# Layers 1 and 2 of a four-layer graph network: another way to the layer norm's scale, a shorter lag, x1 read in pieces; in layer 0, the guess and the diffusion at another place

## The chip, the core and the metric

The kernel runs on one core of one Trainium2 chip. A core has five engines that work side by side, each with its own queue of instructions: TensorE (PE, matrix products; its weight loads have their own queue, PEld), VectorE (DVE), ScalarE (ACT), GpSimd (POOL) and SyncE (SP). SP and POOL issue the DMAs here: SP plain loads and stores, POOL gathers of rows by an index. The metric is the time of one launch on the device in microseconds (us). All times below are in us, counted in a trace from the start of the span, unless marked ns.

## The reference

4096 nodes with 256 features each, and a sparse matrix `adj` (4096 x 4096, a few non-zero entries in a row, the diagonal among them). Four layers, each of the form x = x + layer(relu(layer_norm(x))). Cut to what matters:

```python
# layer 0: two steps of attention (top-p over 4096 logits a row) and of diffusion
for n in range(2):
    A = top_p_attention(Xa, W1, W2, W3)
    Xf = R @ Xf                       # R: adj + I, rows normalised
    Xa = A @ Xa
    Z = Z + Xf @ U1[n].T + Xa @ U2[n].T
out0 = layer_norm(X + Z)
# layer 1: graph convolution
adj_norm = (adj + I) / rowsum
out1 = tanh(adj_norm @ (h @ W) + b)
# layer 2: graph attention with four heads over the non-zero entries
Wh = (h @ W.T).reshape(n, 4, 64)
e = leaky_relu(score_l[:, :, None] + score_r.T[None], 0.2)
alpha = softmax(where(mask, e, -inf), axis=2)
out2 = elu(alpha @ Wh)
# layer 3
out3 = relu(adj @ (h @ weights))
```

The layer norm of a row is (x - mean) / sqrt(var + 1e-5). The kernel applies it as relu(scale * x + shift), with scale = (var + 1e-5) ** -0.5 and shift = -mean * scale.

## The kernel before

The nodes lie in `NB` = 32 blocks of `P` = 128. A block sits with its nodes on the 128 partitions. In the sparse products of layers 1 to 3 a block of targets reads its neighbours in `CHUNKS` = 5 gathers of 128 rows each (`gather`, L835), and PE multiplies them by a compact piece of the matrix, `ac` (`sparse_product`, L850 and L854).

**Order.** On DVE, ACT and PE the program order is the order of execution in the parts considered here (`manual_schedule`). On POOL and SP a scheduler orders the instructions.

**Layer 0** (L793 to L1875). `front` (L1028) computes the normalised input, keys and the moments of the keys. `guess` (L972) is a generator that turns these moments into a first guess of the threshold of every row (`minus_guess`), in pieces that are asked for one at a time: some pieces are a PE product with a DVE operation (list: `near` times `mk`), others four small products, and the last ones short DVE operations (L993 ff). Then `layer0_step(n, ...)` (L1116) gives a `period(b)` for one block of targets. Its text is the table `ORDERS[n]` (L1094): each word is a call, `word@k` a call for block b + k. In a period the logits of block b + 3 (`logits0`, `exps0`: ACT exponentials L1162 with `minus_guess` as their offset), the search for the threshold of block b + 2 (signs, `s1` to `s3`: ACT L1178; updates `r0` to `r3` and `first`: DVE L1190, L1208, L1229), the cut of block b (`below` L1331, `cut` L1393, `drop` L1400, all DVE over 128x4096) and the attention of block b (`flip` PE L1440, `take` ACT L1446, `attend` PE L1455) stand side by side. The word `fill` takes as many pieces of a generator as the tuple `pieces` says for this period (L1853, L1867); periods -3 to -1 are the prologue, in which only b + 2 and b + 3 exist. In step 1 the generator also holds the lists of columns (`listed_columns`, from L794).

In step 1 the diffusion runs as well. `pair(b)` (L1671) names the two blocks which period b mixes: k = 0, the first diffusion, for b = 0 to 15, and k = 1, the second, for b = 17 to 32. `opened` (L1700) starts the gathers of each (`reach`), `mix0` and `mix1` are the sparse products (PE L850, `pr<-vg,ac`), `mixed0` stores a pair (`mixed_d`, L1567) from which the second diffusion gathers. `stood` to `tabled` form layer 1's table `v_d` from the finished blocks; `x1` is stored to `x1_d`.

**Layer 1** (L1877 to L2048). `xr` holds x1 for all 32 blocks and is kept to the end. It is read in eight pieces ahead of everything else of the layer; then the bias and the weights, among them `w_gat`, whose last eight columns DVE computes from tiles of a pool `heads` that closes before the layer's own pools open. In the loop (L2011) a block b is loaded and gathered, and PE forms its sparse product; `y` (DVE L2034), tanh (ACT L2037) and the addition into `xr` follow. Behind it come the class `Projection`'s steps for block o = b - `LAG`, with `LAG` 5: `stats` (mean and variance, and every four blocks the power on POOL, L1934), `shifts` (L1939), `normalise` (ACT relu L1945, PE transposes L1950), `turned` (L1955), `product` (L1961), `store` (`put`, L1986, which writes a block of the table that layer 2 gathers from, through SP).

**Layer 2** (L2050 to L2172). One period per block: `load` gathers five chunks of table rows, `entries(b, k)` forms the factors of a chunk (three heads by ACT, L2079, the fourth by DVE, L2081, then one DVE operation over all four, L2082), `attend` is the product (PE L2097), `attended` copies its sums (ACT L2107), `turned` transposes them, `divided` normalises (DVE L2117, L2119) and takes the exponential for the elu (ACT L2123), `elu` adds to `xr` and takes the stats, and the steps of `Projection` run 8 blocks behind, writing the last layer's table. In a period the exponential stands behind the factors of chunks 0 to 2 and ahead of those of chunks 3 to 5.

**The last layer** (L2186) is a sparse product per block with a relu.

Of the kernel before, what the change touches and what calls it, by code (L numbers as in the profile page):

```python
# [63 lines left out]
F32 = mybir.dt.float32  # L64
# [12 lines left out]
P = 128  # L77
# [577 lines left out]
def fast_layers(  # L655
# [445 lines left out]
    keys@-1 exps1@3 xa_pe@-1 s0@3 mark r0@3 drop copy_xa@-1 s3@2 store_xa@-1 flip0 mark flip1 mark  # L1101
    take0 h_pe@-1 take1 first r3@2 flip2 attend0 mark mark attend1 store_h@-1 take2 flip3 take3 fill
    """,
# [3 lines left out]
    exps1@3 stood@-3 cut mix0 s0@3 laid@-3 s3@2 projected@-3 finish@-1 level@-2 mixed0 drop mix1 tabled@-3  # L1107
    r0@3 r3@2 attend7@-1 shifted@-2 first flip0 spread0 flip1 take0 heads@-1 other1 s1@3 attend0 take1 r1@3 flip2 flip3
    take2 attend1 take3 flip4 attend2 flip5 fill
# [16 lines left out]
    def layer0_step(n, va, kt, own, extra=None):  # L1126
# [544 lines left out]
        def pair(b):  # L1671

            k, i = (0, b) if b < NB // 2 else (1, b - NB // 2 - 1)
            return [(2 * i + r, k) for r in range(2)] if n == 1 and 0 <= b and 0 <= i < NB // 2 else []
# [25 lines left out]
        def opened(b):  # L1700
            if n == 0 and 0 <= b < NB:
                state[b]["adj"] = load_adj(extra, b)
            if n == 1 and b in (0, NB // 2):
                reach(0, b // (NB // 2))
                reach(1, b // (NB // 2))
            if n == 1:
                other(b, 0)
                if 0 < b <= NB:
                    loaded(b - 1, "base", base_d, 1)
                for d in two_ends(b - 1):  # L1710
                    loaded(d, "xb", x, 2)
# [75 lines left out]

        def period(b, fill=(), pieces=(0, 0, 0)):


            pieces = iter(pieces)
            for name, off in tables[max(b - NB + 1, 0)]:
                if name == "fill":
                    some(fill, next(pieces))
                else:
                    calls[name](b + int(off))
# [42 lines left out]
    with ExitStack() as st:  # L1839
# [13 lines left out]
        with tc.manual_schedule(engines=MANUAL):  # L1853
            period, verify, close = layer0_step(0, h0, kt0, own, adj_pool)
            for b in range(-3, NB):
                period(b, guesses, {-3: (3, 0, 0), -2: (3, 9, 9)}.get(b, (0, 0, 0)))
            lists = listed_columns(marks, e_pool.tile([P, N], F32, name="e"), ps)
            guesses = close(lists)

    with ExitStack() as st:  # L1860
# [3 lines left out]
        with tc.manual_schedule(engines=MANUAL):  # L1864
            period, verify, close = layer0_step(1, va1, kt1, s1, vg_pool)
            fill = by_turns(guesses, lists)
            pieces = {-3: (6, 0, 0), -2: (6, 4, 1), -1: (0, 2, 99)}  # L1867
            for b in range(-3, NB + 2):
                period(b, fill, pieces.get(b, (0, 0, 0)))
                if b == -1:  # L1870
# [10 lines left out]
    MANUAL = {ENGINES.DVE, ENGINES.Activation, ENGINES.PE}  # L1881
    GROUP = 4

# [5 lines left out]

    res = ctx.enter_context(tc.tile_pool(name="res", bufs=1))  # L1890
    xr = res.tile([P, NB, D], F32, name="xr")
    for q in range(8):
        bs = slice(q * NB // 8, (q + 1) * NB // 8)
        nc.sync.dma_start(xr[:, bs, :], blocks(x1_d)[:, bs, :])

# [6 lines left out]

    bias = across(res, gcn_b, "bias")
    w_last = weights(res, last_w, "w_last")

    w_gat = res.tile([P, DC, D + 2 * HEADS], F32, name="w_gat")
    nc.sync.dma_start(w_gat[:, :, :D], gat_wt.rearrange("(c p) m -> p c m", p=P))
    with tc.tile_pool(name="heads", bufs=1) as hp:
        for k, a_d in enumerate((gat_al, gat_ar)):
            a_all = across(hp, a_d, f"a_all{k}")  # L1910
            prod = hp.tile([P, DC, HEADS, DK], F32, name=f"prod{k}")
            for c in range(DC):
                nc.vector.tensor_mul(prod[:, c].rearrange("p h d -> p (h d)"), w_gat[:, c, :D], a_all)
                nc.vector.tensor_reduce(
                    w_gat[:, c, D + k * HEADS : D + (k + 1) * HEADS], prod[:, c], AX.X, ALU.add
                )

    class Projection:


        def __init__(self, sm, wk, ps, w, put, width=D):
            self.sm, self.wk, self.ps, self.w, self.put, self.width = sm, wk, ps, w, put, width
            self.tiles = {}

        def stats(self, b):

            six = self.sm.tile([P, 6], F32, name="six")
            nc.vector.bn_stats(six, xr[:, b, :])
            nc.vector.bn_aggr(spread_[:, b, :], six)
            if b % GROUP == GROUP - 1:  # L1930
                bs = slice(b + 1 - GROUP, b + 1)
                var = self.sm.tile([P, GROUP], F32, name="var")
                nc.vector.tensor_scalar_add(var, spread_[:, bs, 1], LN_EPS)
                nc.gpsimd.tensor_tensor(scale[:, bs], var, minus_half[:, :GROUP], op=ALU.pow)  # L1934

        def shifts(self, b):
            if b % GROUP == 0:
                bs = slice(b, b + GROUP)
                nc.vector.scalar_tensor_tensor(  # L1939
                    shift[:, bs], spread_[:, bs, 0], -1.0, scale[:, bs], op0=ALU.mult, op1=ALU.mult  # L1940
                )
# [37 lines left out]
    with ExitStack() as st:  # L1979
# [28 lines left out]

        second = Projection(sm, wk, ps, w_gat, put, D + 2 * HEADS)
        LAG = 5  # L2010
        with tc.manual_schedule(engines=MANUAL):  # L2011
            for b in range(NB + LAG + 3):
                o = b - LAG
                if b < NB:
                    ac = adj_pool.tile([P, CHUNKS + 1, P], F32, name="ac")
                    nc.sync.dma_start(ac, adjc_d[b])
                    vg = gathered(adj_pool, v_d[0], b)
                if 0 <= o < NB:
                    second.shifts(o)
                    second.normalise(o)  # L2020
# [31 lines left out]
    with ExitStack() as st:  # L2052
# [4 lines left out]
        ps = st.enter_context(tc.tile_pool(name="gatps", bufs=2, space=PSUM))  # L2057
        third = Projection(sm, wk, ps, w_last, to_table(wk, v_d[1]))
        state = [{} for _ in range(NB)]
        LAG = 8  # L2060

# [8 lines left out]
        def entries(b, k):  # L2070
# [5 lines left out]
            for h in range(HEADS):  # L2076
                by = s["tab"][:, k, HW + h : HW + h + 1]
                if h < HEADS - 1:
                    nc.scalar.mul(u[:, k, h, :], t[:, h, :], by)  # L2079
# [34 lines left out]
        def divided(b):  # L2114
# [5 lines left out]
                s["y"], s["po"][:, :, :DK], rden.to_broadcast([P, HEADS, DK]), op=ALU.mult  # L2120
            )
            s["below"] = wk.tile([P, D], F32, name="below")
            nc.scalar.activation(s["below"], s["y"].rearrange("p h d -> p (h d)"), AF.Exp)  # L2123
# [10 lines left out]
        with tc.manual_schedule(engines=MANUAL):  # L2134
            for b in range(NB + LAG + 2):
# [10 lines left out]
                if 0 <= o < NB:  # L2146
                    third.shifts(o)
                    third.normalise(o)
# [14 lines left out]
                if turning:  # L2163
                    divided(b - 2)
                if entered:
                    for k in range(3, CHUNKS + 1):
                        entries(b, k)
                if 0 <= o - 2 < NB:
                    third.store(o - 2)
# [95 lines left out]
```

## Time and profile before

| | us |
|---|---|
| median of 3 runs (3387.29 to 3389.24) | 3388.16 |
| the profiled execution | 3391.82 |
| its span in the trace | 3390.0 |
| step 0, first to last period | about 161 to 1279 |
| step 1 | 1404 to 2562 |
| layer 1 | 2562 to 2851 |
| layer 2 | 2851 to 3180 |
| last layer | 3180 to 3390 |

The stages are cut by the trace: the first DVE operation L1331 of a step, the last store of `v_d`, the first gather of layer 2 (2851.22) and the first of the last layer (3179.60). Over the span PE is busy 77%, DVE 78%, ACT 66%, POOL 38%; the mean granted PE clock is 0.89 of full.

How such a page is read: a line of a group names the code line, the engine, the operation, out<-in with shapes and the count; then its busy time in us and the mean ns of one; then the idle time of the engine just before these instructions, with what ended it. "issue" is idle time for which the profile shows no wait. Busy shares over the whole span are means over stages that have different limits, so the stages are looked at one by one, with windows (busy time of each engine in a stretch).

### The profile page before, as it was taken

Reading aid. Unit: us, or ns where it says so; the run is one execution under the profiler, and the core shown is the slowest. Engines: PE = TensorE matmul, PEld = TensorE weight load, DVE = VectorE, ACT = ScalarE, POOL = GpSimd, SP = SyncE. Lnnn points to the kernel's source line nnn. Section 1 sums busy time; section 2 is a strip of 40 time slices with the busy share of each in tenths; the row PEclk is TensorE's granted clock in tenths of the full one; section 3 lists DMA queues with packets and bytes.
Section 4 is the critical chain, followed back from the end, with each engine's and each line's share of the span. In section 5 each row is a group of like instructions: output and inputs, shape, how many; then the busy total and the mean of one; then the engine's idle time right before and its main releaser. Section 6 shows DMA issues by size and latency. Waiting matters only on the chain. (4 is left out here: it accounts for less than half of the span.)

```text
span 3390.0 us, 43724 instructions
## 1 busy us (share of the span) xinstructions
PE 2616.5 (77%) x12404; PEld 1964.9 (58%) x12404; DVE 2652.4 (78%) x9355; ACT 2233.8 (66%) x3340; POOL 1280.6 (38%) x1350
## 2 busy tenths in 40 slices
PE   6558788787887878379898989898883576888666
PEld 5335565565565656157676666767662455777543
DVE  3489999999999998879999999999852344888300
ACT  3588888888888862878888888898620113677200
POOL 1000000000000000188888745656554773754376
PEclk9779899899898999689999999999996898889888
DMA  3012222222222222234444422433335563543475
GB/s 116 8 60 72 81 77 72 87 76 70 88 72 76 82 72 66 76 113 123 133 122 124 123 84 84 124 98 120 100 89 190 166 192 90 135 126 108 139 212 166
DMA packets 213847, 357.00 MB, mean 105 GB/s; under 512 B 33879, under 2 KB 147036, under 8 KB 213596
## 3 DMA queue, kind: packets, MB, share of 16 engines
q1 hardware_dynamic: 169100, 237.74, 22.4%
q0 software_dynamic: 43520, 116.14, 13.0%
q8 instruction: 101, 1.65, 0.2%
q14 instruction: 150, 1.23, 0.1%
q10 hardware_dynamic: 976, 0.23, 0.0%
HBM read 290.85 MB, written 63.13 MB: 104 GB/s over the span
## 5 line engine op out<-in xcount | busy, mean ns | idle before, releaser
L1178 ACT ACTIVATE unread<-e,next_pair 128x4096 uint8<-128x4096 f32 (+1 forms) x384 | 1097.0, 2857 | 46.5 <-DVE next_pair L1229 42.6
L1455 PE MATMUL pa<-va,at 128*128 128x256 f32 x2048 | 501.5, 393 | 71.9 <-DVE t L1585 59.3
L1446 ACT COPY at<-pat 128x512 f32<-128x512 f32 x512 | 291.3, 581 | 310.4 <-PE pat L1440 305.2
L1455 PEld LDWEIGHTS pa<-va,at 128*128 128x128 f32 x2048 | 386.6, 196 | 154.9 <-ACT at L1446 59.2
L1455 PE MATMUL pa<-h,at 128*128 128x256 f32 x2048 | 471.1, 380 | 1.0 <-ACT at L1446 0.8
L1440 PE MATMUL pat<-ident,e 128*128 128x128 f32 x2048 | 319.5, 298 | 192.0 <-DVE e L1400 191.7
L1341 POOL COPY eighth<-best 128x16 f32<-128x16 f32 x64 | 21.7, 339 | 1149.4 <-DVE best L1339 929.8
L1440 PEld LDWEIGHTS pat<-ident,e 128*128 128x128 f32 x2048 | 275.9, 156 | 276.1 <-DVE e L1400 219.3
L1339 DVE MAX8 best<-near 128x8 f32<-128x256 f32 x1024 | 404.3, 416 | 3.2
L1455 PEld LDWEIGHTS pa<-h,at 128*128 128x128 f32 x2048 | 376.2, 191 | 49.0 <-ACT at L1446 4.9
L835 POOL DMA_INDIRECT vg<-v_d,column x320 | 306.7, 959 | 139.4 <-issue 89.7
L1148 PE MATMUL pl<-kt,qb 64*128 64x512 f32 x1024 | 280.5, 660 | 89.9 <-ACT e L1162 89.6
L1162 ACT ACTIVATE e<-pl,minus_guess 128x1024 f32<-128x1024 f32 x256 | 283.4, 1115 | 58.1 <-PE pl L1148 57.7
L850 PE MATMUL acc<-vg,ac 128*128 128x256 f32 x768 | 233.9, 452 | 109.0 <-DMA vg<-v_d,column 81.8
L1331 DVE SCALAR_TENSOR_TENSOR near<-e,end_hi 128x4096 f32<-128x4096 f32 x64 | 286.6, 4478 | 0.1
L1393 DVE SCALAR_TENSOR_TENSOR e<-e,end_t 128x4096 f32<-128x4096 f32 x64 | 286.6, 4478 | 0.0
L1400 DVE MATCH_REPLACE8 e<-drop,e 128x4096 f32<-128x4096 f32 x64 | 282.1, 4408 | 0.0
L850 PEld LDWEIGHTS acc<-vg,ac 128*128 128x128 f32 x768 | 162.1, 225 | 176.8 <-DMA vg<-v_d,column 112.3
L2097 PE MATMUL acc<-u,tabg 128*65 128x128 f32 x1536 | 210.4, 293 | 62.4 <-DVE u L2082 61.1
L835 POOL DMA_INDIRECT ac<-in_adjt,adj_row x160 | 238.6, 1491 | 46.5 <-issue 35.5
L835 POOL DMA_INDIRECT vg<-mixed_d,column x160 | 220.2, 1376 | 92.5 <-issue 44.3
L850 PE MATMUL pr<-vg,ac 128*128 128x257 f32 (+1 forms) x768 | 195.4, 405 | 58.5 <-issue 28.4
(543 smaller groups left out, 4543.9 us busy)
## 6 DMA issues: line engine op xcount, KB each, us to landing
adj<-in_adjt SPq DMA_DIRECT2D x128, 512.0 KB
ac<-adjc_d SPq DMA_DIRECT2D x96, 384.0 KB
adjc_d<-ac SPq DMA_DIRECT2D x32, 384.0 KB
vg<-v_d SPq DMA_DIRECT2D x64, 128.0 KB
targets<-steep_d SPq DMA_DIRECT2D x32, 256.0 KB
vg<-v_d,column POOLq DMA_INDIRECT x320, 3.6
table_d<-tab SPq DMA_DIRECT2D x32, 132.0 KB
tabg<-table_d SPq DMA_DIRECT2D x32, 132.0 KB
```

The lines of the kernel that those rows point to most:

```text
L835: nc.gpsimd.indirect_dma_start(out, None, rows, bass.IndirectOffsetOnAxis(ap=index, axis=0))
L850: nc.tensor.matmul(acc, ac[:, k, :], v[:, k, :], start=(k == 0), stop=(k == CHUNKS and not own))
L1148: nc.tensor.matmul(pl[:, r, :], s["qb"][rows], kt[rows, j * 512 : (j + 1) * 512], start=True, stop=True,)
L1162: nc.scalar.activation(s["e"][:, j * 1024 : (j + 1) * 1024], pl.rearrange("p r c -> p (r c)"), AF.Exp, bias=minus_guess[:, b : b + 1], acc ...
L1178: nc.scalar.activation(unread[:, :width], s["e"][:, :width], func, bias=s["at"], scale=-1.0, accum_out=s["signs"] if func == AF.Sign else ...
L1331: nc.vector.scalar_tensor_tensor(near, s["e"], end["hi"][:, b : b + 1], s["e"], op0=ALU.is_lt, op1=ALU.mult, accum_out=s["low"])
L1339: nc.vector.max(best[:, k, :], near[:, k * (N // SEG) : (k + 1) * (N // SEG)])
L1393: nc.vector.scalar_tensor_tensor(s["e"], s["e"], last, s["e"], op0=ALU.is_ge, op1=ALU.mult, accum_out=s["held"])
L1400: nc.vector.match_replace(s["e"][:, ::-1], s["drop"], s["e"][:, ::-1], 0.0)
L1440: nc.tensor.transpose(pt[:, k, :], s["e"][:, c * P : (c + 1) * P], ident)
L1446: nc.scalar.copy(at, s["pt", g])
L1455: nc.tensor.matmul(s["pa"], s["at", g][:, k, :], va[:, c, :D], start=(c == 0), stop=(c == NB - 1))
```

## The change

In layer 0, both tables `ORDERS` get one more `fill`, ahead of `first`, and the tuples `pieces` become one longer: the pieces that period -3 took at its first `fill` (step 0) or at the first (step 1) are now taken at the new one, which stands behind the logits and the exponentials. `pair` begins the first diffusion at b = 1 and ends it at b = 16, and `opened` starts the gathers of the second one period later.

In layers 1 and 2: the bias and the weights come first and all live in the pool `res`, so the pool `heads` is gone; x1 is read in pieces of four blocks inside layer 1's loop, two pieces at its start and then one every four blocks. `Projection` takes a `group`. With group 1 (layer 1) the scale of a block is formed at once on DVE: a first value by two integer operations and three Newton steps of three operations each, and the shift right behind; nothing of it is on POOL. `LAG` is 2 instead of 5. With group 2 (layer 2) the power stays on POOL, for two blocks at a time instead of four; `shifts` is called for the next block behind `divided`; `LAG` is 6 instead of 8. In `entries` the fourth head's factor of chunks 0 and 3 is formed by ACT. The exponential of the elu becomes `risen`, behind all factors of the period.

```diff
@@ -1101,3 +1101,3 @@
     keys@-1 exps1@3 xa_pe@-1 s0@3 mark r0@3 drop copy_xa@-1 s3@2 store_xa@-1 flip0 mark flip1 mark
-    take0 h_pe@-1 take1 first r3@2 flip2 attend0 mark mark attend1 store_h@-1 take2 flip3 take3 fill
+    take0 h_pe@-1 take1 fill first r3@2 flip2 attend0 mark mark attend1 store_h@-1 take2 flip3 take3 fill
     """,
@@ -1107,3 +1107,3 @@
     exps1@3 stood@-3 cut mix0 s0@3 laid@-3 s3@2 projected@-3 finish@-1 level@-2 mixed0 drop mix1 tabled@-3
-    r0@3 r3@2 attend7@-1 shifted@-2 first flip0 spread0 flip1 take0 heads@-1 other1 s1@3 attend0 take1 r1@3 flip2 flip3
+    r0@3 r3@2 attend7@-1 shifted@-2 fill first flip0 spread0 flip1 take0 heads@-1 other1 s1@3 attend0 take1 r1@3 flip2 flip3
     take2 attend1 take3 flip4 attend2 flip5 fill
@@ -1672,3 +1672,3 @@
 
-            k, i = (0, b) if b < NB // 2 else (1, b - NB // 2 - 1)
+            k, i = (0, b - 1) if b <= NB // 2 else (1, b - 1 - NB // 2)
             return [(2 * i + r, k) for r in range(2)] if n == 1 and 0 <= b and 0 <= i < NB // 2 else []
@@ -1702,3 +1702,3 @@
                 state[b]["adj"] = load_adj(extra, b)
-            if n == 1 and b in (0, NB // 2):
+            if n == 1 and b in (0, NB // 2 + 1):
                 reach(0, b // (NB // 2))
@@ -1787,3 +1787,3 @@
 
-        def period(b, fill=(), pieces=(0, 0, 0)):
+        def period(b, fill=(), pieces=(0, 0, 0, 0)):
 
@@ -1855,3 +1855,3 @@
             for b in range(-3, NB):
-                period(b, guesses, {-3: (3, 0, 0), -2: (3, 9, 9)}.get(b, (0, 0, 0)))
+                period(b, guesses, {-3: (0, 0, 3, 0), -2: (3, 9, 9, 9)}.get(b, (0, 0, 0, 0)))
             lists = listed_columns(marks, e_pool.tile([P, N], F32, name="e"), ps)
@@ -1866,5 +1866,5 @@
             fill = by_turns(guesses, lists)
-            pieces = {-3: (6, 0, 0), -2: (6, 4, 1), -1: (0, 2, 99)}
+            pieces = {-3: (0, 0, 6, 0), -2: (6, 4, 0, 1), -1: (0, 2, 0, 99)}
             for b in range(-3, NB + 2):
-                period(b, fill, pieces.get(b, (0, 0, 0)))
+                period(b, fill, pieces.get(b, (0, 0, 0, 0)))
                 if b == -1:
@@ -1881,3 +1881,2 @@
     MANUAL = {ENGINES.DVE, ENGINES.Activation, ENGINES.PE}
-    GROUP = 4
 
@@ -1890,6 +1889,17 @@
     res = ctx.enter_context(tc.tile_pool(name="res", bufs=1))
+    bias = across(res, gcn_b, "bias")
+    w_last = weights(res, last_w, "w_last")
+
+    w_gat = res.tile([P, DC, D + 2 * HEADS], F32, name="w_gat")
+    nc.sync.dma_start(w_gat[:, :, :D], gat_wt.rearrange("(c p) m -> p c m", p=P))
+    for k, a_d in enumerate((gat_al, gat_ar)):
+        a_all = across(res, a_d, f"a_all{k}")
+        prod = res.tile([P, DC, HEADS, DK], F32, name=f"prod{k}")
+        for c in range(DC):
+            nc.vector.tensor_mul(prod[:, c].rearrange("p h d -> p (h d)"), w_gat[:, c, :D], a_all)
+            nc.vector.tensor_reduce(
+                w_gat[:, c, D + k * HEADS : D + (k + 1) * HEADS], prod[:, c], AX.X, ALU.add
+            )
+
     xr = res.tile([P, NB, D], F32, name="xr")
-    for q in range(8):
-        bs = slice(q * NB // 8, (q + 1) * NB // 8)
-        nc.sync.dma_start(xr[:, bs, :], blocks(x1_d)[:, bs, :])
 
@@ -1902,17 +1912,2 @@
 
-    bias = across(res, gcn_b, "bias")
...
     class Projection:
@@ -1920,3 +1915,4 @@
 
-        def __init__(self, sm, wk, ps, w, put, width=D):
+        def __init__(self, sm, wk, ps, w, put, group, width=D):
+            self.group = group
             self.sm, self.wk, self.ps, self.w, self.put, self.width = sm, wk, ps, w, put, width
@@ -1926,2 +1922,3 @@
 
+
             six = self.sm.tile([P, 6], F32, name="six")
@@ -1929,11 +1926,23 @@
             nc.vector.bn_aggr(spread_[:, b, :], six)
-            if b % GROUP == GROUP - 1:
-                bs = slice(b + 1 - GROUP, b + 1)
-                var = self.sm.tile([P, GROUP], F32, name="var")
-                nc.vector.tensor_scalar_add(var, spread_[:, bs, 1], LN_EPS)
-                nc.gpsimd.tensor_tensor(scale[:, bs], var, minus_half[:, :GROUP], op=ALU.pow)
+            if b % self.group < self.group - 1:
+                return
+            bs = slice(b + 1 - self.group, b + 1)
+            var = self.sm.tile([P, self.group], F32, name="var")
+            nc.vector.tensor_scalar_add(var, spread_[:, bs, 1], LN_EPS)
+            if self.group > 1:
+                nc.gpsimd.tensor_tensor(scale[:, bs], var, minus_half[:, : self.group], op=ALU.pow)
+                return
+            y, t = scale[:, bs], self.sm.tile([P, 1], F32, name="t")
+            bits = self.sm.tile([P, 1], U32, name="bits")
+            nc.vector.tensor_scalar(bits, var.bitcast(U32), 1, None, op0=ALU.logical_shift_right)
+            nc.vector.tensor_scalar(y.bitcast(U32), bits, -1.0, 1597463007.0, op0=ALU.mult, op1=ALU.add)
+            for _ in range(3):
+                nc.vector.tensor_mul(t, y, y)
+                nc.vector.scalar_tensor_tensor(t, t, -0.5, var, op0=ALU.mult, op1=ALU.mult)
+                nc.vector.scalar_tensor_tensor(y, t, 1.5, y, op0=ALU.add, op1=ALU.mult)
+            self.shifts(b)
 
         def shifts(self, b):
-            if b % GROUP == 0:
-                bs = slice(b, b + GROUP)
+            if b % self.group == 0:
+                bs = slice(b, b + self.group)
                 nc.vector.scalar_tensor_tensor(
@@ -2008,4 +2017,4 @@
 
-        second = Projection(sm, wk, ps, w_gat, put, D + 2 * HEADS)
-        LAG = 5
+        second = Projection(sm, wk, ps, w_gat, put, 1, D + 2 * HEADS)
+        LAG = 2
         with tc.manual_schedule(engines=MANUAL):
@@ -2013,2 +2022,6 @@
                 o = b - LAG
+                if b % 4 == 0 and b < NB:
+                    for c in (0, 4) if b == 0 else (b + 4,):
+                        if c < NB:
+                            nc.sync.dma_start(xr[:, c : c + 4, :], blocks(x1_d)[:, c : c + 4, :])
                 if b < NB:
@@ -2018,3 +2031,2 @@
                 if 0 <= o < NB:
-                    second.shifts(o)
                     second.normalise(o)
@@ -2057,5 +2069,5 @@
         ps = st.enter_context(tc.tile_pool(name="gatps", bufs=2, space=PSUM))
-        third = Projection(sm, wk, ps, w_last, to_table(wk, v_d[1]))
+        third = Projection(sm, wk, ps, w_last, to_table(wk, v_d[1]), 2)
         state = [{} for _ in range(NB)]
-        LAG = 8
+        LAG = 6
 
@@ -2077,3 +2089,3 @@
                 by = s["tab"][:, k, HW + h : HW + h + 1]
-                if h < HEADS - 1:
+                if h < HEADS - 1 or k % 3 == 0:
                     nc.scalar.mul(u[:, k, h, :], t[:, h, :], by)
@@ -2121,2 +2133,5 @@
             )
+
+        def risen(b):
+            s = state[b]
             s["below"] = wk.tile([P, D], F32, name="below")
@@ -2146,3 +2161,2 @@
                 if 0 <= o < NB:
-                    third.shifts(o)
                     third.normalise(o)
@@ -2164,2 +2178,4 @@
                     divided(b - 2)
+                if 0 <= o + 1 < NB:
+                    third.shifts(o + 1)
                 if entered:
@@ -2167,2 +2183,4 @@
                         entries(b, k)
+                if turning:
+                    risen(b - 2)
                 if 0 <= o - 2 < NB:
```

## The prediction

> **What bounds the kernel now.** I read the page's slices first, to see which engine is full where.
>
> ```profile
> ## 2 busy tenths in 40 slices
> PE   6558788787887878379898989898883576888666
> DVE  3489999999999998879999999999852344888300
> ACT  3588888888888862878888888898620113677200
> POOL 1000000000000000188888745656554773754376
> ```
>
> A slice is 84.75 us. Slices 2 to 15 and 18 to 28 are layer 0's steps: VectorE (DVE) is full. Slices 30 to 33 are layer 1 (2562 to 2851 us), with no full engine; 34 to 37 layer 2 (2851 to 3180), with three at 6 to 8 tenths; the rest is the last layer. The chain of waits covers only the last layer, so I cut the span into windows instead.
>
> ```profile
> 1411.00:1458.00 47.00, 16.02 (x46) 7.35 (x42) 40.50 (x165) 37.04 (x36) 25.92 (x21) 0.61 0.20 58
> 1700.00:1920.00 220.00, 197.69 (x954) 152.60 (x954) 213.75 (x830) 192.68 (x219) 179.73 (x148) 0.98 0.43 123
> ...
> 2640.00:2760.00 120.00, 76.11 (x326) 59.16 (x325) 49.67 (x152) 21.72 (x94) 90.73 (x93) 0.89 0.66 184
> 2870.00:2960.00 90.00, 73.74 (x533) 66.49 (x531) 71.43 (x178) 61.70 (x198) 65.75 (x64) 0.87 0.53 140
> ```
>
> Columns: length, busy PE, weight loads, DVE, ACT, POOL (with counts), granted PE clock, DMA share, GB/s. DVE has 97% of step 1's middle. In layer 1 POOL comes nearest with 76%; a gather's busy 0.95 is followed by about 0.30 of issue before the next, 1.25 start to start, so 76% busy is nearly a full queue. Layer 2 has nothing full.
>
> Then the waits, by operation. Layer 1's gathers and their releaser, and the shift:
>
> ```profile
> L835 POOL DMA_INDIRECT vg<-v_d,column x160 | 155.2, 970 | 79.2 <-issue 43.2 <-DVE w_gat L1914 27.3 <-PE acc L854 5.9
> ...
> L1945 ACT ACTIVATE h<-xr,shift,scale 128x256 f32<-128x256 f32 x32 | 18.9, 589 | 34.5 <-DVE shift L1939 34.5
> ```
> ```profile
> L1939 DVE SCALAR_TENSOR_TENSOR shift<-spread__23437,scale x16: 130/156/165, 2633.2 to 3169.4; 128x4 f32<-128x4 f32 x16
> ...
>   POOL scale L1934: 22.6, 2
> ```
>
> POOL stands 27.3 before layer 1's first gather, for weights prepared in a pool whose space the gathers reuse; and the projections wait for shifts, which wait for POOL's power (L1934), the first of which stood behind 40 gathers. Layer 2's groups, 31 periods:
>
> ```profile
> L2079 ACT ACTIVATE u<-targets,tabg 128x128 f32<-128x128 f32 x540 | 163.6, 388 | 0.0
> ...
> L2082 DVE SCALAR_TENSOR_TENSOR u<-u,masks 128x512 f32<-128x512 f32 x180 | 125.1, 695 | 51.8 <-ACT u L2079 36.0 <-DVE u L2081 0.5
> L2081 DVE TENSOR_SCALAR u<-targets,tabg 128x128 f32<-128x128 f32 x180 | 52.0, 289 | 0.7 <-PE acc L2097 0.4 <-issue 0.3
> ...
> L2123 ACT ACTIVATE below<-y 128x256 f32<-128x256 f32 x31 | 12.9, 417 | 79.4 <-DVE y L2119 79.4
> ```
>
> ACT idles 79.4/31 = 2.56 a period ahead of the exponential, and DVE 36.0/31 = 1.16 for ACT's factors: the two take turns. The stop is one a period: behind y (L2119) the pair L2081, L2082 takes 1.44 from start to start, elsewhere 0.385. Last, the start of step 1: what the mixing matmuls (L850, 1440 to 1470 us) and a DVE operation of the next signs (L1208, 1400 to 1500) stood idle for.
>
> ```profile
>   DMA vg<-far_d,column: 11.1, 6
> ```
> ```profile
>   ACT unread L1178: 9.1, 1
> ```
>
> **What the Trainium skill says.** "TensorE: Matmul & The Clock Gate" (What's actually happening) gives the array half its clock after an idle window of about 3.4 us. The trace agrees in layer 1: after 3.3 us idle a transpose takes 0.69 and a projection 1.97; after 1.58 idle 0.44 and 1.06. "DMA: Bandwidth & Descriptors" (Anatomy of one DMA — SWDGE (gpsimd) path) puts a fixed cost of about 2.0 us on a transfer, whatever its size; gathers here land a median 3.6 after issue, so a late gather can't be made up. "VectorE: DVE Perf Modes" (The TRN2 errata) says that small operations pay a fixed cost; 128x1 and 128x4 operations here take 0.156 (L1939) to 0.204 (L1208), so Newton's price is a count of instructions.
>
> **The change part by part** (us; sums against the profiled execution, 3391.82).
>
> *Guess behind logits.* In step 0's prologue `minus_guess` is ready at 111.3 and the exponentials start at 113.45. Three pieces leave the place ahead, so the guess should come about 4 earlier. But these three now stand before the update (L1190, 118.5) on DVE, four operations of L993 with them, so the next block's signs start at about 121.0 instead of 122.6: gain 1.6 (0 to 4). In step 1's prologue the moved six pieces (about 1.2 of DVE each) do the same: exponentials about 7 earlier, but L1190 later by 1.6: −1.6 (−3 to +2). Together 0: DVE carries the same work on the path either way.
>
> *Diffusion a period later.* Period 1 of step 1 lasts 47.0 (1453.1 to 1500.0) where its neighbours take about 33. The mixing matmuls (L850) of the first pair stand ahead of the next block's flips on PE and wait to 1462.95 for gathers that POOL issued only from 1426.5. Begun a period later, they find their gathers landed: gain 47.0 − 33.1 = 13.9. The price comes at the hand-over from the first diffusion to the second, which `opened` now starts in period 17. It gathers what period 16 stores; the last store goes out 8.0 into a period, the first gather can start near +10.6, and DVE's 4.48-us operations (L1393, L1331) hold a gather for up to 4.6 beside them. The second mixing then ends at about +30 instead of +28, and the last matmul of the old block stands behind it: 2 (0 to 5). One more period with a mixing before the hand-over: 0.5 to 1. Net gain 11 (7 to 14). The last pair now ends in period 32, which has no new block to feed: hidden.
>
> *Layer 1.* (a) Start. The last v_d store is issued at 2561.99; between layers 1 and 2 such a store (2848.26) was followed by the first gather 2.96 later. So the first gather starts at 2564.95, not 2582.06: gain 17.1. The weights' preparation on DVE (2.7) moves beside the first gathers. (b) POOL. Eight powers, each 1.05 + 0.18, and the stalls around them leave: 160 gathers × 1.252 = 200.3 where now 214.2 pass: gain 13.9. x1 in pieces (8 of 512 KB) adds 4.2 MB to 200 us, 21 GB/s on 184 at 0.66 DMA share: hidden. (c) Behind the last gather. It starts at 2796.3, but layer 2's first gather at 2851.22, 54.9 later: 32.9 to the last y (L2034, 2829.2), since the loop lost about 13 at its first shift (DVE idle 10.9, PE 14.2) and then ran 3 × 6.04 + 9.07 = 27.2 per four blocks, and 22.0 from there, as the projections lag by five blocks. After: landing 3.6, the last sparse product and y, 5.4 in sum, 2 more for order; then two blocks behind it, 8.6 (Newton 2.6, relu 0.6, transposes 0.4, copy 0.4, product 1.1, copies and store 0.8, and the block ahead 2.7) and 2.96 to the gather: 19.0. Gain 36. Newton costs 13 operations × 0.195 (between the two durations above) = 2.55 of DVE per block; with 3.2 before, 5.76 per block, under POOL's 6.26. It is hidden while POOL paces; uncovered it would be 32 × 2.5 = 80. Sum 67; I take 65 for leftover waits (45 to 72).
>
> *Layer 2.* A period is 9.42 (sums L2107, 2870.3 to 3162.3, 31 periods). DVE fills 9.42 − 1.06 (1.44 − 0.385) = 8.36 of it. Two products of L2081 go, 0.386 each to the next start: −0.77; variance and shift come every two blocks rather than four: +0.15. That makes 7.74. ACT fills 61.7/90 × 9.42 = 6.5 to 6.9 and gains two multiplications at about 0.30: 7.5. PE is busy 73.74/90 × 9.42 = 7.7 at the clock of 0.87 granted. The exponential behind the factors takes the 2.56 idle out of ACT's path, and with it DVE's stop. Three engines at 7.5 to 7.7 that feed each other don't run at the largest: 8.0 (7.7 to 8.6). Gain 31 × 1.42 = 44 (25 to 53). What is late next: the normalised block, whose exponential comes about 2 later in a period, covered by the lag. POOL: 8 more powers × 1.2 = 10 over 248, with 6.45 + 0.6 a period, hidden. The tail, 3162.3 to 3179.6, loses two blocks of lag: 3.
>
> The last layer is 160 gathers at 1.25: unchanged. Sum: 0 + 11 + 65 + 44 + 3 = 123. Profiled 3391.82 − 123 = 3269; the median lies 3.66 under the profiled execution, so 3388.16 − 123 = 3265.
>
> **The rivals.**
> *Half of it.* Layer 2 falls to 8.6 only, since PE (7.7, more at a lower clock) or ACT takes DVE's place (25), and layer 1's chain with Newton in it (6.04 + about 0.9) is longer than POOL's 6.26, so that its end is 22 later (43). With 11 and 3: 82, 3306. For it: DVE's shift is now on the way from y to the next block's relu. Against: two blocks of lag cover 12 us.
> *More.* Layer 2 at 7.7 (53), layer 1 in full (70), no hand-over cost (14), tail 4: 141, 3247.
> *Slower.* PE falls to half clock in layer 1 and stays there, as a loop paced by gathers leaves it gaps. A cold cycle was sparse 5.97 + transposes 0.69 + product 1.76 + y, tanh and relu 1.7 = 10.1 (2634.5 to 2642.0 and the waits around). Then 32 × 10.1 = 323 and the tail 35 from 2565: layer 2's first gather at 2923, 72 late; −72 + 11 + 44 + 3 = −14, 3402. It decides from a cycle of about 9.7, where the loss eats the other 58. Against it: PE stayed warm with 1.58 idle per 6.04, and the new loop leaves 6.26 − 4.7 = 1.56.
> *It doesn't do what it says:* the guess moves gain nothing (in the forecast already).
>
> **How the numbers follow.** Forecast 0.60 (own range 3247 to 3285), half 0.21, more 0.12, slower 0.05, and 0.02 for something near no change. 0.2%, 6.8 us, is what a measurement tells from no change. The range 3238 to 3308 takes in most of half and more and leaves out about 0.17. Faster 0.93, same 0.02, slower 0.05.
>
> **What would show it.** Right: step 1's period 1 at about 33; period 17 up to 5 longer; layer 1's first gather 3 after the last v_d store; layer 2's first gather near 2770 on the new clock (2784 − 11 to 14); sums 8.0 apart. Wrong: DVE idle ahead of the shift or ACT's relu in layer 1 (Newton in the path), a granted clock under 0.7 there, or ACT waiting for y in layer 2 still.

## The result, and the profile after

The changed kernel takes 3263.69 us (median of 4 runs, 3261.02 to 3265.84), the kernel before 3388.31 beside it: a ratio of 0.9632, 95% interval 0.9615 to 0.9649. Forecast were 3265 and 3238 to 3308. The profiled execution's span went from 3390.0 to 3263.7. (The four runs of the kernel before are the three of the table above and one more, 3388.46.) The same slices of the page, 81.6 us each now:

```profile
## 2 busy tenths in 40 slices
PE   6558878887887887838989898898987576798766
DVE  3489999999999999789999999999984587799300
ACT  3588888888888883389888888899862122799200
POOL 1000000000000000047888874656655575776476
```

Layer 1 is now in slices 31 to 33, with DVE at 5 to 8 tenths in place of 2 to 4; layer 2 is in 34 to 36, with ACT at 7 to 9. Where the 126 went, by the starts of the same instructions in both traces (us; the forecast's three rows of layer 1 are its sum of 67, of which it took 65):

| stretch | before | after | difference | forecast |
|---|---|---|---|---|
| start to step 0's first L1331 | 161.2 | 157.7 | -3.5 | -1.6 |
| step 0's last L1331 to step 1's first | 125.9 | 129.3 | +3.4 | +1.6 |
| from there to the last store of v_d | 1157.4 | 1142.1 | -15.2 | -11 |
| to layer 1's first gather | 20.1 | 5.3 | -14.8 | -17.1 |
| layer 1's gathers, first to last | 213.3 | 201.0 | -12.3 | -13.9 |
| last gather to layer 2's first | 55.9 | 20.6 | -35.3 | -36 |
| to the first sums | 19.1 | 18.6 | -0.5 | 0 |
| 31 periods of layer 2 | 291.9 | 246.9 | -45.0 | -44 |
| last sums to the last layer's first gather | 17.3 | 14.7 | -2.6 | -3 |
| last layer | 210.4 | 209.9 | -0.6 | 0 |

The windows of the changed kernel, with the columns of before: step 1's period 1, the middle of layer 1, the middle of layer 2.

```profile
1451.00:1487.00 36.00, 30.47 (x141) 23.80 (x140) 32.05 (x124) 30.90 (x33) 23.92 (x24) 0.89 0.35 97
2600.00:2740.00 140.00, 103.86 (x476) 78.70 (x475) 113.72 (x497) 29.90 (x136) 106.20 (x111) 1.00 0.69 204
2880.00:2960.00 80.00, 72.06 (x600) 65.70 (x599) 73.37 (x185) 77.33 (x248) 60.63 (x58) 1.00 0.56 160
```

In layer 1 DVE is busy 81% and PE has its full clock (0.89 before). In layer 2 ACT is busy 97% and DVE 92%; the view of waits names none of DVE's in this window, so what DVE idles there are short gaps between its instructions. Both are full now. The groups of layer 1 that answer to those of before, and three of layer 2:

```profile
L835 POOL DMA_INDIRECT vg<-v_d,column x160 | 153.6, 960 | 61.2 <-issue 43.3 <-DMA a_all<-in_gat_al 12.8 <-DMA vg<-v_d,column 5.2
...
L1954 ACT ACTIVATE h<-xr,shift,scale 128x256 f32<-128x256 f32 x32 | 18.7, 586 | 1.4 <-DVE shift L1948 1.4
```
```profile
L2091 ACT ACTIVATE u<-targets,tabg 128x128 f32<-128x128 f32 x600 | 178.6, 390 | 2.1 <-DMA tabg<-table_d,column 2.1
...
L2094 DVE SCALAR_TENSOR_TENSOR u<-u,masks 128x512 f32<-128x512 f32 x181 | 125.3, 692 | 14.2 <-ACT u L2091 1.7
...
L2138 ACT ACTIVATE below<-y 128x256 f32<-128x256 f32 x31 | 12.8, 414 | 10.9 <-DVE y L2131 10.7
```

The relu's wait for the shift fell from 34.5 to 1.4. It shows in the y's (L2034 before, L2046 after, one a block): before, two steps from one y to the next took 20.7 and 21.5, each with a shift that waited for POOL's power (22.6 together), and five later ones 9.1 to 9.5; after, none behind the third is over 6.8. From first to last y it took 232.1 before and takes 192.3. ACT's idle time ahead of the exponential fell from 79.4 to 10.9, and DVE's wait for ACT's factors from 36.0 to 1.7.

The 7.96 of layer 2 is a mean. From the ninth sums on a period takes 7.79 (9.52 before); one earlier period takes 16.2, since DVE waits there for the first power that POOL makes for the shift. In layer 2 that power is still on POOL, and it stood behind POOL's gathers:

```profile
L1948 DVE SCALAR_TENSOR_TENSOR shift<-spread__23449,scale x48: 149/159/175, 2571.1 to 3046.2; 128x1 f32<-128x1 f32 x32, 128x2 f32<-128x2 f32 x16
...
  POOL scale L1933: 7.8, 1
```

The mixing matmuls of step 1's first pair, between 1440 and 1500 us, in the changed kernel:

```profile
L850 PE MATMUL pr<-vg,ac x24: 377/380/484, 1475.6 to 1482.4; 128*128 128x257 f32 x24
...
  issue: 1.8, 2
  PE pr L854: 1.4, 1
```

They run through; the 11.1 of waiting for gathers is gone.

### The profile page after: what moved, and what is told of

It is laid out like the page before. It is cut to its first block, busy times and chain, and to the rows that moved or that the text cites. A ratio compares the mean times of both kernels' runs of the same rounds, so it can differ in the third digit from the quotient of the medians.

```text
span 3263.7 us, 44120 instructions
## 1 busy us (share of the span) xinstructions
PE 2569.4 (79%) x12404; PEld 1926.0 (59%) x12404; DVE 2699.1 (83%) x9707; ACT 2250.3 (69%) x3404; POOL 1273.2 (39%) x1350
## 3 DMA queue, kind: packets, MB, share of 16 engines
q14 instruction: 152, 1.25, 0.1%
## 5 line engine op out<-in xcount | busy, mean ns | idle before, releaser
L1178 ACT ACTIVATE unread<-e,next_pair 128x4096 uint8<-128x4096 f32 (+1 forms) x384 | 1097.0, 2857 | 63.2 <-DVE next_pair L1229 57.8
L1455 PE MATMUL pa<-va,at 128*128 128x256 f32 x2048 | 496.0, 390 | 59.8 <-DVE t L1585 47.3
L1455 PEld LDWEIGHTS pa<-h,at 128*128 128x128 f32 x2048 | 376.4, 191 | 48.9 <-ACT at L1446 5.0
L1162 ACT ACTIVATE e<-pl,minus_guess 128x1024 f32<-128x1024 f32 x256 | 283.3, 1114 | 45.1 <-PE pl L1148 35.4
L850 PE MATMUL acc<-vg,ac 128*128 128x256 f32 x768 | 227.2, 442 | 93.5 <-DMA vg<-v_d,column 74.0
L1331 DVE SCALAR_TENSOR_TENSOR near<-e,end_hi 128x4096 f32<-128x4096 f32 x64 | 286.8, 4481 | 0.1
L835 POOL DMA_INDIRECT vg<-far_d,column x160 | 255.1, 1594 | 60.2 <-issue 42.4
L2109 PE MATMUL acc<-u,tabg 128*65 128x128 f32 x1536 | 193.2, 280 | 43.2 <-DVE u L2094 42.7
```

Source lines behind the costliest of these rows:

```text
L835: nc.gpsimd.indirect_dma_start(out, None, rows, bass.IndirectOffsetOnAxis(ap=index, axis=0))
L850: nc.tensor.matmul(acc, ac[:, k, :], v[:, k, :], start=(k == 0), stop=(k == CHUNKS and not own))
L1162: nc.scalar.activation(s["e"][:, j * 1024 : (j + 1) * 1024], pl.rearrange("p r c -> p (r c)"), AF.Exp, bias=minus_guess[:, b : b + 1], acc ...
L1178: nc.scalar.activation(unread[:, :width], s["e"][:, :width], func, bias=s["at"], scale=-1.0, accum_out=s["signs"] if func == AF.Sign else ...
L1331: nc.vector.scalar_tensor_tensor(near, s["e"], end["hi"][:, b : b + 1], s["e"], op0=ALU.is_lt, op1=ALU.mult, accum_out=s["low"])
L1455: nc.tensor.matmul(s["pa"], s["at", g][:, k, :], va[:, c, :D], start=(c == 0), stop=(c == NB - 1))
```

## The experiments

Each run is the changed kernel with the edit shown. They fell on three chips. On one the kernel before took 3384.08, near the 3388.31 of the result; on the two others 3612.09 and 3612.50, and there the stages that gather nodes are longer (below). Each run is therefore held against a run of the changed kernel on a like chip; on the slower kind there is one such run, the measure below, on the second of the two chips.

**Layer 2: the exponential and the shares, and layer 1: Newton.** These four ran together; the kernel before took 3384.08 beside them. First the measure, unchanged:

> The changed kernel once more, as the measure for the runs beside it on the same chip (the kernel before took 3612 us on the chip of the four runs ahead of this, 3388 on the first one). On a chip like the first: 3264, periods of layer 2 7.96 apart, y's of layer 1 6.2 apart. On one like the second: near 3520, the stages in which nodes are gathered longer, layer 2's periods still near 8.

3264.09, ratio 0.9642 (0.9626 to 0.9658). Layer 2's period is 7.97 in the mean and 7.79 from the ninth sums on, and layer 1's y's are 6.26 apart from the fifth on (so also below).

*The exponential back.*

```diff
                 if turning:
                     divided(b - 2)
+                    risen(b - 2)
...
-                if turning:
-                    risen(b - 2)
```

> The changed kernel with the elu's exponential back between the factors of chunks 2 and 3; ACT keeps the fourth head of chunks 0 and 3. Theory (the exponential made ACT wait for y and DVE then for ACT): ACT idles 2.2 to 2.6 a period ahead of it again, and as ACT is now full the period grows by about that, 7.96 to 9.5 or 10: +48 to 65 on the changed kernel. Rival (the share between ACT and DVE carries the gain): period under 8.5, +15 at most.

3307.12, ratio 0.9770 (0.9754 to 0.9787): 43 slower than the measure, a little less than the 48 expected. The sums are 9.38 apart, in the mean and from the ninth on. Two groups of layer 2 in this run:

```profile
L2094 DVE SCALAR_TENSOR_TENSOR u<-u,masks 128x512 f32<-128x512 f32 x180 | 125.0, 694 | 62.1 <-ACT u L2091 48.9 <-issue 0.5 <-DVE u L2093 0.5
...
L2138 ACT ACTIVATE below<-y 128x256 f32<-128x256 f32 x31 | 12.9, 417 | 64.4 <-DVE y L2131 64.4
```

Both waits are back: 64.4 of ACT for y and 48.9 of DVE for ACT. ACT and DVE take turns again. Against the kernel before, with two products more on DVE, the period is 9.52 - 9.38 = 0.14 shorter from the ninth sums on (9.42 - 9.38 = 0.04 in the mean).

*The fourth head all on DVE.*

```diff
-                if h < HEADS - 1 or k % 3 == 0:
+                if h < HEADS - 1:
```

> The changed kernel with the fourth head's factor of every chunk on DVE again; the exponential stays behind the factors. Theory (DVE becomes the bound with 7.74 + 0.77 = 8.5): period 8.5, +17. Rival (ACT, which is at 97% now, is relieved by 0.58 and DVE has room): period 7.8 or less, -5 or more.

3288.76, ratio 0.9715 (0.9699 to 0.9732): 25 slower than the measure, where 17 was expected; the period is 8.73 in the mean and 8.63 from the ninth sums on. The window of 80 us in layer 2, columns as above, and its two groups:

```profile
2880.00:2960.00 80.00, 67.50 (x532) 59.32 (x531) 71.73 (x188) 62.91 (x200) 49.94 (x50) 0.98 0.51 138
```
```profile
L2094 DVE SCALAR_TENSOR_TENSOR u<-u,masks 128x512 f32<-128x512 f32 x181 | 125.6, 694 | 19.3 <-ACT u L2091 0.5
...
L2138 ACT ACTIVATE below<-y 128x256 f32<-128x256 f32 x31 | 12.9, 415 | 47.9 <-DVE y L2131 47.9
```

DVE waits 0.5 for ACT, while ACT (79% busy) waits 47.9 for DVE's y: DVE is the bound by itself. The two products cost 8.63 - 7.79 = 0.84 a period, no less than their own time on DVE (2 × 0.386 = 0.77), and relieving ACT won nothing back: DVE had no room left in the changed kernel. From the ninth sums on, then, the exponential's place is worth 9.52 - 8.63 = 0.89 a period, and the share 0.84 on top of it, but 0.14 without it. The 0.89 and the 0.14 are differences to the kernel before, which also has the longer lag and the power for four blocks; no run separates these from the exponential's place and the share.

*Six Newton steps.*

```diff
-            for _ in range(3):
+            for _ in range(6):
```

> The changed kernel with six Newton steps instead of three in layer 1: nine more operations of 128x1 a block on DVE, 1.75 us. Theory (three steps are hidden by little: DVE 5.76 a block under POOL's 6.26; six aren't): y's 7.5 apart instead of 6.2, layer 1 about 40 longer than the changed kernel on the same chip (less where gathers pace it at over 7). Rival (the projection's lag of two blocks hides it all): no change over 5.

3304.49, ratio 0.9765 (0.9749 to 0.9782): 40 slower than the measure. The y's are 7.45 apart, and the last stands 38.8 behind the last gather (5.4 in the measure). Its window in layer 1, and what DVE's y (L2046) waited for in it, first in the changed kernel, then in this run:

```profile
2600.00:2740.00 140.00, 94.52 (x392) 73.36 (x391) 122.73 (x580) 25.34 (x114) 104.02 (x110) 0.91 0.66 190
```
```profile
  PE acc L854: 13.7, 22
```
```profile
  PE acc L854: 0.5, 2
```

DVE is busy 88% where three steps had 81%, the rest being gaps between instructions. The operations of a Newton step start 0.194 apart in the trace, so nine more are 1.75 us; they moved the period by 1.19, so 0.56 of room was there. The changed kernel shows it: DVE's wait of 13.7 for PE's product over 22 y's is 0.62 a block, and with six steps it is gone. The forecast's 5.76 of DVE a block under 6.26 is right within about 0.1, and Newton is hidden only by that margin.

**The parts on the slower chips.** The kernel before took 3612.09 and 3612.50 beside the two groups of runs there. The measure:

> The changed kernel once more, as the measure for the runs beside it: 0.964 of the kernel before on a chip like the first, 129.3 between the steps, first gather of layer 1 5.1 behind the store.

3517.38, ratio 0.9743 (0.9727 to 0.9758): a gain of 95 rather than 125. Step 1's periods 2 to 15 take 571 together (452 on the first chip) and the y's of layer 1 are 7.39 apart, the last 35 behind the last gather. Step 0, which has no gathers, takes 1117.8 from its first L1331 to its last (1117.6 there). All gathers of v_d in this run, both layers, and what POOL waited for (with 36 of the diffusion ahead of them), show it:

```profile
L835 POOL DMA_INDIRECT vg<-v_d,column x320: 942/949/1308, 2688.9 to 3494.7; - x160
...
  issue: 106.2, 320
  remote: 47.3, 15
```

A gather's busy time is the same 0.949; the added idle time (47.3, `remote` in the view) has an end that the profile can't name. Layer 2's mean period, 7.99, is like the first chip's, but made otherwise: most of its periods take 8.07, and none is long.

*The guess.*

```diff
-    r0@3 r3@2 attend7@-1 shifted@-2 fill first flip0 spread0 flip1 take0 heads@-1 other1 s1@3 attend0 take1 r1@3 flip2 flip3
+    r0@3 r3@2 attend7@-1 shifted@-2 first flip0 spread0 flip1 take0 heads@-1 other1 s1@3 attend0 take1 r1@3 flip2 flip3
...
-            pieces = {-3: (0, 0, 6, 0), -2: (6, 4, 0, 1), -1: (0, 2, 0, 99)}
+            pieces = {-3: (6, 0, 0), -2: (6, 4, 1), -1: (0, 2, 99)}
...
```

> The changed kernel with step 1's pieces of the guess back at their old place; step 0's stay at the new one. Theory (the piece costs DVE the same wherever it stands, and behind the exponentials it holds up the update L1190): from step 0's last L1331 to step 1's first it took 125.8 us before and 129.3 after; this run shows 125.8 again and is 3.5 us faster than the changed kernel, near 3260. Rival (those 3.5 us come from the gathers that now start a period later): 129.3 stays, 3264.

3516.75, ratio 0.9738 (0.9720 to 0.9756). The stretch between the steps is 125.8, where the runs on chips of this kind with the pieces at their new place have 129.3 (one of them 127.3): the loss between the steps is the guess's own. ACT's idle time there shows why an earlier start isn't a gain; the signs (L1178) and the exponentials (L1162) between 1275 and 1420 us, first of this run, then of the measure:

```profile
L1178 ACT ACTIVATE unread<-e,next_pair 128x4096 uint8<-128x4096 f32 (+1 forms) x12 | 34.3, 2854 | 6.2 <-DVE next_pair L1229 5.9
...
L1162 ACT ACTIVATE e<-pl,minus_guess 128x1024 f32<-128x1024 f32 x12 | 13.3, 1110 | 12.3 <-PE pl L1148 12.1
```
```profile
L1178 ACT ACTIVATE unread<-e,next_pair 128x4096 uint8<-128x4096 f32 (+1 forms) x11 | 30.6, 2777 | 15.0 <-DVE next_pair L1229 14.8
...
L1162 ACT ACTIVATE e<-pl,minus_guess 128x1024 f32<-128x1024 f32 x12 | 13.3, 1112 | 6.3 <-PE pl L1148 6.2
```

With the new place ACT idles 6 less ahead of the exponentials and 9 more ahead of the signs, which wait for DVE's update; the stretch is 3.5 longer. The total is the measure's within the intervals, so that the 3.5 reach the end is not shown.

*The diffusion.*

```diff
-            k, i = (0, b - 1) if b <= NB // 2 else (1, b - 1 - NB // 2)
+            k, i = (0, b) if b < NB // 2 else (1, b - NB // 2 - 1)
...
-            if n == 1 and b in (0, NB // 2 + 1):
+            if n == 1 and b in (0, NB // 2):
```

> The changed kernel with pair and opened as before, so the first diffusion begins in period 0 again. Theory: period 1 of step 1 is at 47 us again (+12), periods 2 to 16 lose the 6 us that they have gained, period 17 gets back its 4, step 1 ends 15 later: 3279. Rival (the gain in periods 2 to 16 isn't the diffusion's): +9, 3273.

> The kernel of diffusion_back again, where the chip allows it beside the changed kernel on a chip like the first. Theory: period 1 at 47, periods 2 to 16 6 us longer, period 17 4 or less shorter: +13 to +16 on the changed kernel. Rival: +9.

3544.08 (0.9813, 0.9796 to 0.9829) and 3543.41 (0.9804, 0.9789 to 0.9819): 26 slower than the measure, where 13 to 16 was expected for a chip like the first. Period 1 takes 72.7 in both, 42.5 in the measure. The mixing matmuls' waits between 1440 and 1540 us, in the second of these runs:

```profile
  DMA vg<-far_d,column: 17.7, 7
```

The measure shows no such wait. The mechanism holds; it is larger here, where gathers take longer. Periods 2 to 16 take 601.6 and 604.4, the measure 603.6: going back cost nothing there, where 6 was expected. The gain that the changed kernel has in them on the first chip isn't tested by these runs.

*Layer 1's old projections.*

```diff
-        second = Projection(sm, wk, ps, w_gat, put, 1, D + 2 * HEADS)
-        LAG = 2
+        second = Projection(sm, wk, ps, w_gat, put, 4, D + 2 * HEADS)
+        LAG = 5
...
                 if 0 <= o < NB:
+                    second.shifts(o)
                     second.normalise(o)
```

> The changed kernel with layer 1's projections as before: POOL's power for four blocks, shifts ahead of the relu, lag 5; the weights first and x1 in pieces stay. Theory (Newton and the lag carry what layer 1 gained behind its first gather, the order of the loads only the earlier start): first gather still 5 us behind the last v_d store, but layer 2's first gather about 269 us behind layer 1's first one instead of 221.5: +48, 3311. Rival (the stall at the first shift came with the late start and goes with it): the 21 us steps in the y's are gone, +20 to 30, 3285 to 3293.

> The kernel of pow4_lag5 again, beside the changed kernel. Theory: +40 to +48, from the y's (7.75 apart instead of 6.2), the place of the last y behind the last gather (some 34 instead of 5) and the tail (22 instead of 15). Rival: +20 to +30, without the 21 us steps of the y's.

3528.94 (0.9763, 0.9747 to 0.9780) and 3525.91 (0.9761, 0.9746 to 0.9776): 9 to 12 slower than the measure, with intervals that overlap its own, far from both theories. The y's are 7.85 and 7.71 apart (7.39 in the measure), the last 34 behind the last gather (35), and one step of 15.7 and 14.5 is left of the two of 21. The tail, from the last y to layer 2's first gather, is 19.7 instead of 14.85. In all, layer 1 takes 294.1 and 289.8 from its first gather to layer 2's first one, 284.8 in the measure. Layer 2 gives nothing back: from its first gather to its last sums it takes 283.5 and 283.8 (283.1). Since the y's end some 34 behind the last gather here in either form, these runs can't say how Newton and the lag share the gain on the first chip. The first gather stays 5.2 behind the last store, so the earlier start needs neither of them: it belongs to the order of the loads and to the pools.

*The lag alone.*

```diff
         second = Projection(sm, wk, ps, w_gat, put, 1, D + 2 * HEADS)
-        LAG = 2
+        LAG = 5
```

> The changed kernel with a lag of 5 instead of 2 in layer 1, Newton on DVE kept. Theory (the lag only sets the tail): y's 6.2 us apart as now, from the last y to layer 2's first gather 22 instead of 14.8: +7, 3271. Rival (with a lag of 2 the scale and shift sit in the loop's chain, and a longer lag frees it): the y's come closer, the tail is 7 longer, and the sum is 0 or below.

3526.11, ratio 0.9755 (0.9734 to 0.9777): 9 slower than the measure, with overlapping intervals (7 was expected). The tail is 19.95 instead of 14.85, 1.7 a block of lag; the y's are 7.48 apart, no closer than 7.39. The lag sets the tail, and a longer one shows no gain in the loop.

*A version meant to beat the changed one.* The guess of step 1 at its old place, as above, and the last layer's weights later:

```diff
-    w_last = weights(res, last_w, "w_last")
+    w_last = res.tile([P, DC, D], F32, name="w_last")
...
+                    if b == 8:
+                        nc.sync.dma_start(w_last, last_w.rearrange("(c p) m -> p c m", p=P))
```

> The changed kernel with step 1's pieces of the guess at their old place, and the last layer's weights loaded at block 8 of layer 1 rather than ahead of the last v_d store. Theory: 125.8 instead of 129.3 between the steps (-3.5), layer 1's first gather about 4 behind the last store instead of 5.1 (-1): 3259 to 3260 on a chip like the first. Rival (the time between the steps is given back in step 1, the store's landing doesn't depend on the loads): 3264.

3516.35 (0.9726, 0.9709 to 0.9742) beside the measure's 3517.38: no difference outside the intervals. The stretch between the steps is 125.9, and layer 1's first gather comes 4.86 behind the store (4.97). This doesn't show that the loads ahead of the store cost nothing: SP issued the load of `w_gat`, of the same 256 KB, in the place of that of `w_last`, just ahead of the store:

```profile
2685.22 0.43 SPq L1894 DMA_DIRECT2D w_gat<-in_gat_wt  x1
2685.74 0.42 SPq L1669 DMA_DIRECT2D v_d<-v  x1
```

It ran on the slower kind of chip alone.

## Why the prediction was right

**The total** was forecast at 123 and is 126 in the traces (124.6 between the medians). Every part that was forecast to change moved that way and none is off by more than 4.3, but that the sum comes so close is partly luck: a gain of 6.7 in step 1 and one of 1.8 at the start, which the working doesn't have, stand against terms that fell short.

**Layer 2** was forecast at 8.0 a period and is 7.96 in the mean. The reasons hold: two engines took turns, and the exponential's place made them. The size is right by two errors. The step from the engines' own times to 8.0, "three engines at 7.5 to 7.7 that feed each other don't run at the largest", didn't come true: from the ninth sums on the period is 7.79, near DVE's own 7.74, with ACT at 77.33/80 × 7.79 = 7.53 (7.5 forecast). And POOL's powers, taken as hidden, cost one stop of 7.8 at the first shift, as they had in layer 1 before. The gains don't add as the working had them either: it summed 1.06 for the stop and 0.77 for the products; measured are 0.89 for the place, with the lag and the group, then 0.84 for the products, and 0.14 for the products without the place.

**Layer 1.** The first gather was taken at 2.96 behind the store, from the transition between layers 1 and 2; it is 5.26. That term was too favourable by 2.3. The trace names a load of `a_all` as the last release. No run took away the loads that SP issues around the store, so the cause stays open. POOL's term (13.9) came to 12.3. What stands behind the last gather is 20.6 where 19.0 was said: 5.7 to the last y (7.4 forecast), and 14.8 from there (11.6 forecast). The working lets the last gather start at 2796.3, which is where it ends; it starts at 2795.3. That Newton is covered, the term that carried the rival of a half gain, is shown by doubling it: DVE had about 0.6 of room a block. The rival of a half-clock PE fell: the granted clock in layer 1 is 1.00. How the 47.6 behind the first gather divide among Newton, the lag and the loads was not tested on a chip like the first; the y's and the relu's wait show that the stops for the shift are gone.

**Step 1.** Period 1 fell from 47.0 to 35.2 (11.8), where 13.9 was forecast, and period 0 by 1.6. Period 17 grew by 3.9 in the profiled execution (by 3.7 and three times 0.8 in the later ones on a chip like it); 2 was taken. The 6.7 of periods 2 to 15 weren't in the working. The traces name a wait that went with them: what L1585 on DVE waited for in these periods, before and after.

```profile
  DMA mixed_d<-t: 7.5, 6
```
```profile
  PE pa L1455: 1.0, 4
```

L1585 writes a tile `t` that the stores of the mixed blocks (`mixed_d`) use too; in the changed kernel they no longer hold it up. No run tests this, and on the slower chips neither form has the wait. The working also has DVE's long operations hold a gather for up to 4.6; one beside L1331 took 5.12.

**The guess** was forecast at 0 in sum. In step 0 it won what was forecast: from its first product (L981) to the first L1331 it takes 61.4 before and 59.7 after, 1.7 less, and 59.4 to 59.8 in all other runs, which share this place. The rest of the table's 3.5 lies ahead of L981, which the change doesn't touch:

```profile
L981 PE MATMUL pm<-both,fold x2: 242/246/250, 99.8 to 99.9; 128*128 128x1 f32 x2
```
```profile
L981 PE MATMUL pm<-both,fold x2: 250/260/271, 98.1 to 98.2; 128*128 128x1 f32 x2
```

In the other runs L981 comes at 93.5 to 101.7, so the 1.8 between these two lines is within what executions differ by. Ahead of step 1 the loss of 1.6 became 3.5. The sign was seen from the order of DVE's work, but the size was not: counted from step 0's last L1331, the exponentials start 6.2 earlier, and the update L1190 comes 4.6 later (83.8 to 88.4), where 1.6 was taken. So in sum the guess lost about 1.8.

## What to carry to other kernels

Where two engines take turns, first move the operation that makes one wait for the other's fresh result; shares between them are worth little until then (0.14 against 0.84 a period here). A mean over periods can hide a single stop: 7.96 is 7.79 and one period of 16.2. Price small work put on an engine against the pace of the engine that bounds the loop, and double it to see how much room is left: three Newton steps fitted, six cost 40. A gain in stages that gather need not carry over to another chip: on one where these stages took longer, the same change won 2.6% in place of 3.7%.

## What was not expected of the hardware

On two chips the kernel before took 6.6% longer (3612.09 and 3612.50) than on the chip of the result (3388.31). Of the changed kernel there are traces of both kinds. A gather's busy time on POOL is alike (0.946 and 0.949 median), and so is step 0 (1117.6 and 1117.8); step 1, layer 1 and the last layer, which gather, are longer. The last layer's 160 gathers start over 198.9 on one and 223.2 on the other, 1.25 and 1.40 each. PE's granted clock in the middle of step 0 is 0.91 on both and in that of the last layer 0.84 and 0.70; whether that is a cause or follows from waiting isn't shown. What makes these chips' gathers slower wasn't found.
